# Reordering the prologue of a cross-attention kernel: value-bias sums, weight sums and the banks of the first queries

## The chip, the cores and the metric

The kernel runs on one core of a Trainium2 chip. The metric is device time in microseconds (us), the median of several executions. The engines are TensorE (PE in the profile, with PEld for its weight loads), VectorE (DVE), ScalarE (ACT), GpSimd (POOL) and SyncE (SP, which here only issues DMAs). Each engine works through its own queue in order, and semaphores hold an instruction until its data are there.

## The reference

One layer: layer norm, cross-attention with 8 heads of 64, a small recurrent state over time, and a row that is added at the end. All of it is float32.

```python
# builder_state x: (1, 4096, 512), base_state: (1, 3202, 512), program_probs: (1, 3202, 64)
x = _layernorm(builder_state, g1, beta1)
base_n = _layernorm(base_state, g1, beta1)
x = residual + _mha(x, base_n, W_qkv, b_qkv, W_o, b_o)   # softmax(q k^T / 8) v, 8 heads
xn = _layernorm(x, g2, beta2)
U = (xn @ W_in.T + b_in) @ Bmat
s = jax.nn.silu(s @ A.T) + u_t                           # a scan over the 4096 steps
x = x + einsum('tbs,sh->bth', states, Cmat)
return x + (program_probs.mean(axis=1) @ W_prog.T + b_prog)[:, None, :]
```

The gain g1 and the shift beta1 of the first layer norm are folded into the weights. For keys, values and queries each weight is multiplied by g1, and beta1 times the weight, summed over its rows, goes into the bias.

## The kernel before, in words

The work has a prologue and a main stage. The prologue makes all keys and values of the 3202 context rows, writes them to DRAM (`kd`, `vd`), makes the constants, and makes the first queries. The main stage goes over 8 blocks of 512 queries, 4 pairs of heads and 2 halves, and for each over 13 double chunks of keys: scores (L1067), exponential (L1144), sum (L1152), product with the values (L1201). The change is in the prologue, and nothing of the main stage's code is touched.

**Chunks and groups.** The context is cut into 26 chunks of 128 rows, loaded as `cx` (L426). A chunk is normalised: statistics on DVE (L267, L269), factors on POOL (L276, L278, L280), scaling on ACT (L288); for the first two chunks DVE scales (L440). It is then turned, by PE and a copy (L304, L456) or, for chunks 0 and 1 of groups 2 to 5, by DVE and DMAs (L407, L419). Chunks 0 to 3 make group 0, whose values (L540) and keys (L663) are plain products, one of values for each chunk and one of keys for each pair of heads. The groups 1 to 5 use a seven-product scheme for keys and values alike (`Seven`, L500): it needs sums of the weights, made once on POOL (`weight_sums`, L708, tiles `sk` and `sv`), and four differences of the turned chunks for each group, made on DVE (`t`, L735). Results are kept by ACT (L513, L517) and joined by DVE (the pieces named `tied`, L523).

**Bias sums.** `shift(k, after, due)` makes the bias of queries (k = 0), keys (1) or values (2). DVE multiplies the raw weight by beta1 and adds up four row blocks (L399 once, L402 three times; pieces `("wv", 0)` to `"wv.w"` for the values). PE sums over rows with eight one-column matmuls (L801, piece `"wv.pb"`), and DVE adds the given bias (L808, `"wv.bias"`). The keys' bias is needed when a key product is copied out (L673). The values' bias is needed only for `rowv`, a row of the output projection that comes late in the prologue. The gains themselves are L392: those of the values come before the plan starts, those of keys and queries are pieces (`gained`).

**The planner.** The function `lead` lists the prologue as pieces: name, engine, a cost in ns, what must come first (`after`), a due time, and rings of buffers taken and given. `Plan.order` plays the pieces through on a clock of its own. Whenever an engine is free, it takes the ready piece with the earliest due time, and the pieces are then emitted in that order. So `after`, `due` and costs decide the order in each engine's queue; on the chip only data and buffers hold an instruction back. Buffers of tiles that follow one another in a ring do so too: a chunk's load waits until the sixth chunk before it has been normalised.

The planner knows one more rule, the port. A POOL piece, or a DVE piece whose name's first part is in `PORT`, is not started on its clock before the last such piece is over:

```python
def shares(p):
    return p["engine"] == "POOL" or p["engine"] == "DVE" and p["name"][0] in self.PORT

def fits(p):
    if port > now and shares(p):
        return False
```

The due times that matter are: values of chunk c 4000 c, keys of head pair hp in group 0 14500 + 3560 hp, gains of the keys 9500, their bias 11500, statistics of chunks 4 and 5 22500 and their factors 24000, weight sums 9000 (values) and 16000 (keys), the column sum of a bias 4000 after the due time given to `shift`.

**The banks of PSUM.** Small products take their tile from `m_tile`, which goes round a list of pools: `ps_m` and `ps_p` in the prologue, one bank each; `ps_m` and `ps_n` in the main stage. Fourteen tiles come before the first query product in the prologue, which makes three products of the first queries (`heads`, L333, copied by L342): they stand in `ps_m`, `ps_p` and `ps_m`. The main stage begins with `sample` (L1087), which opens a tile in `ps_m` and one in `ps_n`. Its pools are opened after those of the prologue are closed, in the order `ps_s` (scores, four banks), `ps_n`, `ps_o` (two banks, the products with the values; the fourth query product uses the first of them).

Of the kernel before, what the change touches and what calls it, by code (L numbers as in the profile page):

```python
# [55 lines left out]
def keys(c):  # L56


    return CK if c < NCH - 1 else REST
# [11 lines left out]
class Plan:  # L71
# [9 lines left out]
    KEEP, ALONE = 6000, 30000  # L81
    UNIT = ("add", "inverse", "scale", "fall", "join", "output", "sums", "den", "swap", "gather", "fold", "rest")
    ENDS = 2 * NC * NQB - 2
    PORT = ("add", "rest", "fold", "gather", "scale")

    SHIFT = {
        "row.store": 11.5, "fold": 2, "rows.outs": 0.75, "heads": -12, "sample": -3, "spread": 4.75,
# [26 lines left out]
    def order(self):  # L114
# [13 lines left out]
        def shares(p):  # L128
            return p["engine"] == "POOL" or p["engine"] == "DVE" and p["name"][0] in self.PORT

# [61 lines left out]
def xattn_ssm_kernel(  # L192
# [66 lines left out]
    wq = kv.tile([P, NC, H], F32, name="wq")  # L259
# [52 lines left out]
    ps_m = actx.enter_context(tc.tile_pool(name="ps_m", bufs=1, space=PSUM))  # L312
    m_pools = [ps_m]

    def m_tile(shape, name):

        pool = m_pools.pop(0)
        m_pools.append(pool)
        return pool.tile(shape, F32, tag="m", name=name)
# [9 lines left out]
    def heads(Q, hp, xn, home=None):  # L329

        pq = home() if home else m_tile([P, 512], f"pq_{Q}_{hp}")
        for i in range(NC):
            nc.tensor.matmul(  # L333
                pq,
                wq[:, i, hp * P : (hp + 1) * P],
                xn[:, i, :],
                start=(i == 0),
                stop=(i == NC - 1),
            )
        yield  # L340
        t = qp.tile([P, QB], F32, tag="q", name=f"q_{Q}_{hp}")
        nc.scalar.activation(  # L342
            t, pq, AF.Identity, bias=bias[:, hp : hp + 1], scale=HD**-0.5
        )
        qt[Q, hp] = t
# [37 lines left out]
    wk = wp.tile([P, NC, H], F32, name="wk")  # L383
    wv = wp.tile([P, NC, H], F32, name="wv")
# [89 lines left out]
    def quarters(w):  # L474

        lo, hi = slice(0, QU), slice(QU, H)
        return w[:, :2, lo], w[:, 2:, lo], w[:, :2, hi], w[:, 2:, hi]
# [78 lines left out]
    def lead():  # L556
# [6 lines left out]
        add = plan.add  # L563
# [3 lines left out]
        def start_of(g):  # L567
            if g == n_g:
                return start_of(g - 1) + 10000
            return 31000 + (g - 1) * GROUP if g else 0  # L570

        def used(c):
            g, i = divmod(c, GC)
            if g == 0 or g == n_g:
                return start_of(g) + i * 4000
            return start_of(g) + (i > 1) * 4 * SLOT
# [16 lines left out]
        for c in range(1, NCH):  # L593
            u, n, g, v = used(c), keys(c), c // GC, {}
# [101 lines left out]
        def weight_sums(name, w, tags, after, due):  # L696

            a11, a12, a21, a22 = quarters(w)
            left = dict(zip("124", (a11, a12, a22)))
            tiles = {}  # L700

            def sum_(k, x, y, op):
                i = "57".index(k) if k in "57" else "63".index(k)
                if k in "57":
                    tiles[i] = xp_.tile([P, 2, H], F32, tag=tags[i], name=f"s{name}{k}", bufs=1 if name == "k" else 2)
                left[k] = tiles[i][:, int(k in "63")].rearrange("p (c o) -> p c o", c=2)
                x, y = (left[z] if isinstance(z, str) else z for z in (x, y))
                nc.gpsimd.tensor_tensor(left[k], x, y, op)  # L708

            for i, (k, x, y, op) in enumerate((  # L710
                ("5", a21, a22, ALU.add), ("6", "5", a11, ALU.subtract),
                ("7", a11, a21, ALU.subtract), ("3", a12, "6", ALU.subtract),
            )):
                first = {"6": "5", "7": "6", "3": "7"}.get(k)
                add(("s", name, k), "POOL", 1300, partial(sum_, k, x, y, op),
                    after + ([("s", name, first)] if first else []), due + i * 1300)
            return left
# [63 lines left out]
        def weighted_(name, w, by, after, due):  # L781
            v = sv_[name] = {}

            def run(i):
                if i == 0:
                    v["w"] = weighted(w, by, f"shift_{name}")
                v["t"] = next(v["w"])

            for i in range(NC):
                add((name, i) if i < NC - 1 else name + ".w", "DVE", 750 if i else 450, partial(run, i),  # L790
                    [(name, i - 1)] if i else after, due + i, [] if i else ["w"])

        def shift(k, after, due):
            name = "w" + "qkv"[k]
            weighted_(name, raw[k], be1s, after, due)
            v = sv_[name]

            def product():
                v["pb"] = m_tile([P, 512], f"pb_{k}")
                for o in range(NC):  # L800
                    nc.tensor.matmul(  # L801
                        v["pb"][:, o : o + 1], v["t"][:, o * P : (o + 1) * P], ones[:, 0:1],
                        start=True, stop=True,
                    )

            def sum_():
                cs = slice(k * NC, (k + 1) * NC)
                nc.vector.tensor_tensor(bias[:, cs], v["pb"][:, :NC], bqkv[:, cs], ALU.add)  # L808
                if k == 0:
                    nc.vector.tensor_scalar(bias[:, cs], bias[:, cs], HD**-0.5, None, ALU.mult)  # L810

            add(name + ".pb", "PE", 900, product, [name + ".w"], due + 4000, ["m"], [("w", (name, 0))])
            add(name + ".bias", "DVE", 300, sum_, [name + ".pb"], due + 5500, [], [("m", name + ".pb")])
# [3 lines left out]
        def fetched(name, issue, cost, after, due):  # L817
            add("d." + name, "ACT", 100, issue, after, due)
            arrives("in." + name, cost, ["d." + name])
# [5 lines left out]
        def issue(name, src, *shape, tag=None):  # L825
            return lambda: nc.scalar.dma_start(tile_(*shape, name=name, tag=tag), src)
# [6 lines left out]

        gained("wk", 1, wk, 9500)
        shift(1, ["in.wk"], 11500)
        shift(2, [], 18500)
        fetched("win", issue("win", w_in.rearrange("(c p) i -> p c i", p=P), P, NC, H, tag="raw_k"), 6000,
                ["wk.w", ("k", 0, 0)], 17000)
        fetched("bm", issue("bm", bmat.rearrange("(c p) s -> p c s", p=P), P, NC, NS), 1500, [("k", 0, 0)], 17100)
# [108 lines left out]
        for t in range(NT):  # L948
            name, v, d = f"x{t * P}", {}, 96000 + t * 12000
# [24 lines left out]
        for hp in range(FIRST):  # L974
            v, d = {}, start_of(n_g) + 10000 + 3000 * hp

            def head(hp=hp, v=v):
                v["g"] = heads(0, hp, first_xn["xn"])
                next(v["g"])

            add(("h0", hp), "PE", 3560, head,
                [("x.copy", t) for t in range(NT)] + ["wq", "wq.bias"], d, ["m", "q"])
            add(("h0.q", hp), "ACT", 690, lambda v=v: next(v["g"], None), [("h0", hp)], d + 3600, [],
                [("m", ("h0", hp))])
# [3 lines left out]
        for hp in range(NC):  # L988
            keys_(0, hp)
        lefts = [  # L990
            weight_sums("k", wk, ("x1", "xn2"), ["wk"], 16000), weight_sums("v", wv, ("x", "x"), [], 9000),
        ]
        for g in range(1, n_g):
            group(g, lefts)
# [14 lines left out]
    with tc.manual_schedule():  # L1009
        load_chunk(0)  # L1010
        nc.scalar.dma_start(g1s, g1)
        fetch_w(2, nc.scalar, slice(0, NC // 2))
        fetch_w(2, nc.sync, slice(NC // 2, NC))
        load_chunk(1)
        load_chunk(2)
        fetch_w(1, nc.sync)
        load_chunk(3)
        idle = m_tile([P, 512], "idle")
        nc.scalar.copy(bu, neg_half)
        for _ in range(11):  # L1020
            nc.tensor.matmul(idle[:, :P], a_t, a_t, start=True, stop=True)
        for t, src in ((be1s, beta1), (bqkv, b_qkv), (g2s, g2), (be2s, beta2)):
            nc.sync.dma_start(t, src)
        for c in range(4, 6):
            load_chunk(c)
        early = [first_chunk(c) for c in range(2)]
        next(early[0])
        next(early[0])
        turn_chunk(0)
        copy_chunk(0)  # L1030
        gain(2, wv, 0)
        gain(2, wv, 1)
        next(early[1])
        gain(2, wv, 2)
        xhs[2] = normalize(cxs.pop(2), CK, "c2", pool=cin)
        gain(2, wv, 3)
        next(early[1])
        lead()
# [107 lines left out]
    def add(w, c):  # L1146

        nb, t = blocks(c), w["s"][c]
        before = w["s"][0] if c == 1 else w["acc"]
        if c == 1:  # L1150
            w["acc"] = accp.tile([CK, 2, 2, QU], F32, tag="acc", name=f"acc_{w['name']}", bufs=3)
        nc.vector.tensor_tensor(  # L1152
            w["acc"][:, :, :nb, :], t[:, :, :nb, :], before[:, :, :nb, :], ALU.add
        )
# [1176 lines left out]
```

## Time and profile before

| | us |
|---|---|
| median of 3 runs | 1930.76 (1929.99 to 1931.4) |
| the profiled execution, its own time | 1930.1 |
| its span, first to last instruction | 1928.2 |
| PE busy in the span | 1907.7 (99%) |
| DVE busy | 1507.3 (78%) |
| ACT busy | 1173.5 (61%) |
| POOL busy | 227.7 (12%) |
| mean granted TensorE clock | 0.997 of full speed |

The span is what the profile's times are counted in; the profiled execution's own time is 1.9 us longer. Busy shares are an average over a prologue of some 205 us and the main stage after it. In a row of the timeline stand the start, the duration, engine and line, the operation, output and inputs with their shapes, the count, and in brackets the idle time just before with what ended it. Several instructions of a kind may be merged to one row, whose duration then runs from the first to the end of the last. Durations of matmuls contain the pipeline's fill, so the distance between two starts says more than the duration of one row.

### The profile page before, as it was taken

To read this page: it belongs to the slowest core of one execution; us is meant where nothing else is said; L and a number is where in the kernel's file an instruction comes from. 1 tells how busy PE (TensorE), PEld (TensorE's weight loads), DVE (VectorE), ACT (ScalarE), POOL (GpSimd) and SP (SyncE) were. 2 spreads that over 40 slices of the span, in tenths; PEclk is the share of its full clock that TensorE was granted. 3 is DMA by queue.
4 is the path that set the end of the run, shared out by engine and by line. 5 is a ranking of instruction groups with operands and counts; after the bars stand their busy time and mean duration, and the time that the engine had idled before them with its cause. 6 is when DMAs were issued, how large, how long until landed. Compare 5 with 4: busy or idle time off the path is not lost.

```text
span 1928.2 us, 67580 instructions
## 1 busy us (share of the span) xinstructions
PE 1907.7 (99%) x29296; PEld 1325.5 (69%) x29296; DVE 1507.3 (78%) x2035; ACT 1173.5 (61%) x1647; POOL 227.7 (12%) x378
## 2 busy tenths in 40 slices
PE   8999999999999999999999999999999999999997
PEld 4888678676667766666667666766666666766675
DVE  5652588688878887888868887888789886978877
ACT  2342576676656666667657665766666765766653
POOL 5110000001200120011100120012000110011105
PEclk9999999999999999999999999999999999999999
DMA  6654133133422243223413342224323342545577
GB/s 216 184 155 115 44 109 85 48 93 85 126 77 82 87 120 88 71 81 96 113 54 86 91 126 79 82 87 118 81 72 90 81 121 60 149 117 145 173 188 230
DMA packets 260762, 207.47 MB, mean 108 GB/s; under 512 B 94633, under 2 KB 233897, under 8 KB 260461
## 3 DMA queue, kind: packets, MB, share of 16 engines
q1 hardware_dynamic: 256440, 196.48, 35.8%
q10 hardware_dynamic: 4020, 6.62, 1.2%
q8 instruction: 232, 3.80, 0.8%
q14 instruction: 70, 0.57, 0.1%
HBM read 156.32 MB, written 29.88 MB: 97 GB/s over the span
## 4 chain that ended last, share of the span: by engine, by line


## 5 line engine op out<-in xcount | busy, mean ns | idle before, releaser
L1144 ACT ACTIVATE p<-s,shifts 128x1024 f32<-128x1024 f32 (+1 forms) x832 | 892.8, 1082 | 475.4 <-PE s L1067 458.8
L1152 DVE TENSOR_TENSOR acc<-p,acc 128x1024 f32<-128x1024 f32 (+1 forms) x704 | 832.6, 1183 | 135.6 <-ACT p L1144 99.9
L1067 PE MATMUL s<-q,k 64*64 64x256 f32 x12800 | 840.2, 377 | 0.2 <-ACT p L1144 0.2
L1201 PE MATMUL po<-p,v 64*64 64x256 f32 x12800 | 839.3, 377 | 0.0
L1067 PEld LDWEIGHTS s<-q,k 64*64 64x64 f32 x12800 | 502.9, 133 | 196.7 <-ACT p L1144 15.0
L1201 PEld LDWEIGHTS po<-p,v 64*64 64x64 f32 x12800 | 500.4, 133 | 181.8 <-issue 17.3
L1273 DVE RECIPROCAL rd<-rd 128x256 f32<-128x256 f32 (+1 forms) x64 | 110.1, 1722 | 70.8 <-ACT rd L1268 70.8
L1438 POOL TENSOR_TENSOR xr<-xr,rowb 128x512 f32<-128x512 f32 x30 | 40.7, 1365 | 998.4 <-DMA xr<-in_x_dram 608.2
L333 PE MATMUL pq<-xn,wq 128*128 128x512 f32 x248 | 110.5, 598 | 0.0
L1444 PE MATMUL pa<-wo,o 128*128 128x512 f32 x240 | 107.0, 599 | 0.0
L1152 DVE TENSOR_TENSOR acc<-p,p 128x1024 f32<-128x1024 f32 x64 | 78.2, 1222 | 10.1 <-ACT p L1144 9.8
L333 PEld LDWEIGHTS pq<-xn,wq 128*128 128x128 f32 x248 | 45.8, 190 | 55.8 <-issue 55.8
L1444 PEld LDWEIGHTS pa<-wo,o 128*128 128x128 f32 x240 | 44.4, 190 | 56.0 <-issue 56.0
L342 ACT ACTIVATE q<-pq,bias 128x512 f32<-128x512 f32 x31 | 21.3, 687 | 84.3 <-PE pq L333 84.3
L1176 DVE TENSOR_TENSOR acc<-swap,acc 64x256 f32<-64x256 f32 x126 | 55.5, 441 | 9.2 <-ACT swap L1171 7.5
L1171 ACT COPY swap<-acc 64x256 f32<-64x256 f32 x126 | 50.8, 404 | 8.6 <-DVE acc L1159 5.4
L1138 DVE TENSOR_TENSOR acc<-x,acc 2x256 f32<-2x256 f32 x128 | 53.1, 415 | 2.6
L1461 POOL TENSOR_TENSOR xr<-x,modb 128x512 f32<-128x512 f32 x30 | 38.2, 1273 | 120.1 <-DVE x L1457 120.1
L1159 DVE TENSOR_TENSOR acc<-acc 128x512 f32<-128x512 f32 x63 | 44.2, 701 | 1.4
L523 DVE TENSOR_TENSOR ks<-pky,ks 128x512 f32<-128x512 f32 x15 | 10.4, 692 | 43.4 <-PE pky L500 26.4
L1334 POOL TENSOR_SCALAR rstd_x<-mv_x 128x1 f32<-128x1 f32 x28 | 6.2, 220 | 321.3 <-DVE mv_x L1331 319.6
L517 ACT ACTIVATE ks<-pkx,bias 128x256 f32<-128x256 f32 x40 | 16.8, 471 | 42.5 <-PE pkx L500 26.0
(260 smaller groups left out, 1410.1 us busy)
## 6 DMA issues: line engine op xcount, KB each, us to landing
k<-kd SPq DMA_DIRECT2D x432, 128.0 KB, 2.5
v<-vd SPq DMA_DIRECT2D x432, 128.0 KB, 2.2
xn<-x SPq DMA_DIRECT2D x448, 32.0 KB, 1.9
xr<-in_x_dram SPq DMA_DIRECT2D x30, 256.0 KB, 3.1
x1d<-xr SPq DMA_DIRECT2D x30, 256.0 KB, 2.6
x<-in_x_dram SPq DMA_DIRECT2D x28, 256.0 KB, 3.6
cx<-in_ctx_dram SPq DMA_DIRECT2D x25, 256.0 KB, 4.4
kd<-ks SPq DMA_DIRECT2D x20, 256.0 KB, 2.3
```

The lines of the kernel that those rows point to most:

```text
L333: nc.tensor.matmul(pq, wq[:, i, hp * P : (hp + 1) * P], xn[:, i, :], start=(i == 0), stop=(i == NC - 1),)
L1067: nc.tensor.matmul(s[k0 : k0 + HD, a, b, :], kts[(*w["at"][:2], c)][r, b * CK + k0 : b * CK + k0 + HD], q[r], start=True, stop=True, skip_ ...
L1138: nc.vector.tensor_tensor(to[r], t[r], to[r], ALU.add)
L1144: nc.scalar.activation(t[:, :, :nb, :], w["ps"][c][:, :, :nb, :], AF.Exp, bias=w["shift"])
L1152: nc.vector.tensor_tensor(w["acc"][:, :, :nb, :], t[:, :, :nb, :], before[:, :, :nb, :], ALU.add)
L1159: nc.vector.tensor_tensor(acc[:, :, 0, :], acc[:, :, 0, :], acc[:, :, 1, :], ALU.add)
L1171: nc.scalar.copy(w["swap"][r], of[(1 - k) * HD : (2 - k) * HD])
L1176: nc.vector.tensor_tensor(of[r], w["swap"][r], of[r], ALU.add)
L1201: nc.tensor.matmul(w["po"][k][a * HD : (a + 1) * HD, :QU], vts[Q, hp, c][r, b, a * HD : (a + 1) * HD], t[r, a, b, :], start=(c == 0 and b ...
L1273: nc.vector.reciprocal(w["rd"][:, part], (w["pd"] if last else w["rd"])[:, part])
L1438: nc.gpsimd.tensor_tensor(v["x"], v["x"], rowb, ALU.add)
L1444: nc.tensor.matmul(v["pa"], o_t[Q, c, half][:, t * P : (t + 1) * P], wo[:, c, :], start=(c == 0), stop=(c == NC - 1),)
```

## The change

Four edits, all in the planner's inputs for the prologue. First, the names `t`, `tied`, `wk`, `wv`, `wq` and `rowv` join `PORT`: the differences, the joins and the multiply-and-add pieces of the bias sums (all but the last of each four, whose names are plain strings) are kept apart from POOL's pieces on the planner's clock. Second, the value-bias sums come after the first key product, `("k", 0, 0)`, with due time 24000 instead of 18500; before they had no predecessor. Third, the weight sums of the values come after the statistics of chunk 5, due 20000 instead of 9000; before they had no predecessor. Fourth, when the first of the first query products is issued, the list of pools is sorted so that `ps_m` comes last; the three products then stand in `ps_p`, `ps_m` and `ps_p`.

```diff
-    PORT = ("add", "rest", "fold", "gather", "scale")
+    PORT = ("add", "rest", "fold", "gather", "scale", "t", "tied", "wk", "wv", "wq", "rowv")
...
         shift(1, ["in.wk"], 11500)
-        shift(2, [], 18500)
+        shift(2, [("k", 0, 0)], 24000)
...
             def head(hp=hp, v=v):
+                if hp == 0:
+                    m_pools.sort(key=lambda pool: pool is ps_m)
                 v["g"] = heads(0, hp, first_xn["xn"])
                 next(v["g"])
...
-            weight_sums("k", wk, ("x1", "xn2"), ["wk"], 16000), weight_sums("v", wv, ("x", "x"), [], 9000),
+            weight_sums("k", wk, ("x1", "xn2"), ["wk"], 16000), weight_sums("v", wv, ("x", "x"), [("c.stats", 5)], 20000),
```

## Prediction

> **What bounds the kernel now.** I read the page first, for who is busy, then a table of stretches, for where TensorE (PE) is not.
>
> ```profile
> span 1928.2 us, 67580 instructions
> ...
> PE 1907.7 (99%) x29296; PEld 1325.5 (69%) x29296; DVE 1507.3 (78%) x2035; ACT 1173.5 (61%) x1647; POOL 227.7 (12%) x378
> ```
> ```profile
> 13.11:28.20 15.09, 10.08 (x24) 5.38 (x25) 14.59 (x22) 3.51 (x5) 12.24 (x15) 0.77 0.41 112
> ...
> 47.69:195.00 147.31, 147.31 (x719) 122.20 (x718) 66.41 (x124) 51.86 (x96) 20.65 (x60) 1.00 0.53 151
> 195.00:205.00 10.00, 9.13 (x37) 4.98 (x41) 0.68 (x1) 3.17 (x6) 0.37 (x2) 1.00 0.21 59
> 205.00:1928.20 1723.20, 1710.95 (x28426) 1176.03 (x28418) 1411.66 (x1852) 1105.89 (x1525) 180.60 (x267) 1.00 0.36 101
> ```
>
> In the stretches the columns are start and end, length, then busy time of PE, weight loads, DVE (VectorE), ACT (ScalarE) and POOL (GpSimd), granted clock, DMA share, GB/s. PE is busy in all of 47.69 to 195 us and in 1710.95 of the 1723.20 us after 205. So what follows the prologue cannot get shorter by this change; it can only begin earlier. There are two holes the change could touch: 13.11 to 28.20, where PE has 10.08 us of work in 15.09 and the clock is 0.77, and a short one near 204. The waits of PE name both.
>
> ```profile
> PE pb L801 <- DVE shift_wv L402: 5.0, 1, 5.0
> ...
> PE pv L540 <- ACT ct L456: 0.8, 2, 0.5
> ```
> ```profile
> PE sm L1087 <- ACT q L342: 0.9, 1, 0.9
> ```
>
> The timeline shows the first hole (start, duration, instruction).
>
> ```profile
> 10.35 0.73 DVE L440 TENSOR_SCALAR xh_c<-cx,mv_c,rstd_c 128x256 f32<-128x256 f32 x2
> ...
> 11.45 0.60 PE L304 MATMUL tp_c<-ident,xh_c 128*128 128x128 f32 x4
> 11.51 1.27 POOL L708 TENSOR_TENSOR sv<-wv 128x512 f32<-128x512 f32 x1
> ...
> 12.21 0.85 DVE L399 TENSOR_SCALAR shift_wv<-raw_v,be1s 128x512 f32<-128x512 f32 x1 [1.13 <-DMA be1s<-in_L_xattn_beta_dram]
> ...
> 12.45 0.66 PE L304 MATMUL tp_c<-ident,xh_c 128*128 128x128 f32 x4 [0.40 <-ACT xh_c L288]
> ...
> 13.09 4.97 DVE L402 SCALAR_TENSOR_TENSOR shift_wv<-raw_v,be1s,shift_wv 128x512 f32<-128x512 f32 x3
> ...
> 15.81 1.70 POOL L708 TENSOR_TENSOR sv<-wv,sv 128x512 f32<-128x512 f32 x1
> 17.99 0.68 DVE L456 COPY ct<-tp_c 128x512 f32<-128x512 f32 x1
> 18.12 1.87 PE L801 MATMUL pb<-ones,shift_wv 128*128 128x1 f32 x8 [5.01 <-DVE shift_wv L402]
> ...
> 19.85 8.94 PE L540 MATMUL pv<-wv,ct 128*128 128x512 f32 x16
> ```
> ```profile
> 28.63 1.04 PE L304 MATMUL tp_c<-ident,xh_c 128*128 128x128 f32 x8
> ```
>
> PE turns chunks 1 and 2 by 13.11 and then stands until 18.12: next in its queue is the column sum of the value bias (L801). That waits for three DVE instructions that took 4.97 us, and behind them stands the copy of chunk 1 (17.99) that the next values need. Two things stretch the hole. The same three instructions for the queries, with POOL still, took 2.33, against 4.97 beside POOL's sums; and after the pause the clock is half.
>
> ```profile
> 17.00:18.00 1.00, 0.00 (x0) 0.00 (x0) 1.00 (x2) 0.00 (x0) 0.51 (x1) 0.50 0.00 0
> ```
> ```profile
> 33.49 3.60 PE L663 MATMUL pk<-ct,wk 128*128 128x512 f32 x8
> ...
> 36.92 0.95 PE L801 MATMUL pb<-ones,shift_wk 128*128 128x1 f32 x8
> ...
> 37.73 10.55 PE L663 MATMUL pk<-ct,wk 128*128 128x512 f32 x24
> ...
> 39.57 0.48 DVE L399 TENSOR_SCALAR shift_wq<-raw_q,be1s 128x512 f32<-128x512 f32 x1
> ...
> 40.09 2.33 DVE L402 SCALAR_TENSOR_TENSOR shift_wq<-raw_q,be1s,shift_wq 128x512 f32<-128x512 f32 x3
> ```
>
> **The change, part by part.** *Value-bias sums.* They leave the front of the queues: DVE's four (L399, L402) and PE's eight (L801) now come after the first key product. They issue no DMA. What is late next? Chunk 1's copy: its turn ends at 11.45 + 0.60 = 12.05, DVE has been free since 10.35 + 0.73 = 11.08, and 0.68 for the copy gives 12.8; PE is still turning chunk 2 until 13.11. So the values of chunk 1 start at 13.11 instead of 19.85. Eight warm matmuls of this shape take 36.92 - 33.49 = 3.43 us, two chunks 6.87, and chunk 3 can be turned at about 20.0 instead of 28.63: **8.6 us**. The eight column sums come back later, in a stretch where PE is full: 37.73 - 36.92 = **0.8 us** lost. I take no cost for DVE's four: at 0.48 + 2.33 they end long before PE reaches their sum, behind the fourth key product (due time 28,000 against 25,180 for that product). The most they could cost is the rival "early sum" below.
>
> Is chunk 3 there at 20.0, and are the key weights there at 33.49 - 8.6 = 24.9?
>
> ```profile
> 3.29 0.62 SPq L426 DMA_DIRECT2D cx<-in_ctx_dram  x1
> ```
> ```profile
> DMA to landing us min/median/max: 8.7/8.7/8.7
> ```
> ```profile
> 18.59 0.68 DVE L267 BATCH_NORM_STATS2 st_c<-cx 128x6 f32<-128x512 f32 x1
> ...
> 19.30 0.18 DVE L269 BATCH_NORM_AGGREGATE mv_c<-st_c 128x2 f32<-128x6 f32 x1
> ...
> 20.84 0.81 ACT L288 ACTIVATE xh_c<-cx,nmr_c,rstd_c 128x512 f32<-128x512 f32 x1 [7.11 <-POOL nmr_c L280]
> ...
> 21.16 1.64 DVE L392 TENSOR_SCALAR wk<-raw_k,g1s 128x512 f32<-128x512 f32 x4
> ```
>
> Chunk 3 lands at 12.0. From its statistics to the end of its normalising took 18.59 to 21.65, 3.1 us, in a contended place. Begun at 12.8 it ends near 15.9: four us of slack. The DMA engines move nothing at 17 to 18, so everything asked for early, the key weights too, has landed by 17; four gains at 1.64 end by 18.7, six us ahead. Both covers hold; if one failed, each us late would be a us of PE.
>
> *Weight sums.* POOL's four sums of wv (L708) move from 11.5 to behind chunk 5's statistics. By their due times (20,000 for wv, 16,000 for wk) all eight sums pass ahead of chunk 5's factors (24,000), so chunk 5 and those behind it in POOL's queue are made later, and so is SP's load of chunk 11, which waits for chunk 5's buffer. Eight at 1.27 to 1.70 take 10 to 14 us; begun near 16 they end by 30, chunk 5 is normalised by 33 (3.1 as above), and PE wants it after the fourth key product, which ended at 47.69, so at 47.69 - 8.6 = 39.1 or later. Cost nothing, 6 us of cover.
>
> *GpSimd and VectorE exclude each other.* The planner keeps some DVE pieces and all of POOL's apart on its own clock. No wait is added to the program: only orders change. A piece that would be run beside POOL is passed over, and another goes ahead of it. Where they collide the trace puts 4.97 against 2.33, so up to 2.6 us of DVE for three instructions could be gained; PE is full from 28 on, so a gain there is worth nothing. The other side is the rival "t late". I take zero.
>
> [...]
>
> *First queries.* The hole near 204:
>
> ```profile
> 200.41 0.69 ACT L342 ACTIVATE q<-pq,bias 128x512 f32<-128x512 f32 x1 [3.02 <-PE pq L333]
> 203.84 0.69 ACT L342 ACTIVATE q<-pq,bias 128x512 f32<-128x512 f32 x1 [2.75 <-PE pq L333]
> ...
> 204.68 0.78 PE L1087 MATMUL sm<-q,kx 64*64 64x256 f32 x8 [0.87 <-ACT q L342]
> ```
>
> The sample (L1087) uses queries copied long before; it waits for the PSUM bank. Fourteen tiles before them alternate between two banks, so query products 0 and 2 stand in ps_m, which the sample opens first. Swapped, product 2 stands in ps_p and ps_m's reader is the copy at 200.41, over by 201.1. ps_p's bank becomes, by order of allocation, the last of the main stage's (ps_o's second), written only at the first value product. So the wait goes: between 0, if the bank meets another early tile, and **0.87**. I take 0.87.
>
> Sum: 8.6 - 0.8 + 0.87 = 8.7 us. The profiled execution took 1930.1 us (span 1928.2), so 1921.4; the median of the three runs, 1930.76, lies 0.66 above that execution. **Forecast: 1922.1 us.**
>
> **The rivals.** *t late* (chance 0.20). In the five groups PE's products wait for differences that DVE makes (t, L735), with hardly any room:
>
> ```profile
> 113.38 0.69 DVE L735 TENSOR_TENSOR t<-ct 128x512 f32<-128x512 f32 x1
> ```
> ```profile
> 114.13 1.99 PE L500 MATMUL pky<-t,sk 128*128 128x256 f32 x8
> ```
>
> t ends at 114.07, its product begins at 114.13. If the planner holds t back while POOL has a piece, DVE takes statistics first, 0.68 and the aggregate, 0.86 in all. Once in each of five groups is 4.3 us: 1926.4. Against it: POOL is busy in only 20.65 of 147.31 us there, and the planner knows t's new time and can order PE otherwise.
>
> *Not apart after all* (0.12). The program holds no exclusion, so POOL's sums may still fall on DVE's gains or key-bias sums. Fully in turn, one gain and one sum are 0.41 + 1.27 = 1.7 us, four 6.7: key weights at 17 + 6.7 = 23.7 against 24.9, still hidden; with statistics placed between (two at 0.86) 0.5 late. Add as much again for the clock and a lost swap: about 1924.
>
> *Early sum* (0.10, the slow side). PE's column sum of the value bias is placed ahead of the second key product instead of behind the fourth, because in the planner that product isn't ready. PE gets there at 28.3 + 0.8 = 29.1. If DVE has the query gains (1.64) and the query shift (0.48 + 2.33) in front of wv's four (0.85 + 4.97 beside POOL), it ends 10.3 us later: PE stands that long and loses the clock again, which cost 8.78 - 6.87 + 0.92 = 2.8 us in the trace (19.85 to 28.63 for two chunks; 1.87 against 0.95). 1922.1 + 13.1 = 1935. It decides by its place in PE's queue: behind the fourth product PE arrives at 39.4, when 29.1 + 10.3 is just over. Due times speak for the late place; parts of it (a 5 us wait) would end near 1930.
>
> **How the numbers follow.** Forecast 0.58 (its own range 1920.5 to 1924, the lower end if PE's short waits for copies in the first 30 us, 0.8 in all, go too); t late 0.20; not apart 0.12; early sum 0.10. The range to 1927 takes in the first three and leaves early sum and the worst of t late out: 1920.5 to 1927. A measurement of this kernel can tell about 0.2%, 3.9 us, from no change. Below 1926.9 lie forecast, not apart and two thirds of t late: 0.83; within 0.2%: 0.09; slower: 0.08.
>
> **What would show it.** Right: no wait of PE for shift_wv, values of chunk 1 starting near 13.1, clock 1.00 throughout 13 to 28, first key product near 25, group stages full, no wait of sm for q. Then the 205 us mark falls near 196 and the rest lasts the same 1723 us. Wrong: PE waits on t or on shift_wv at a new place; a clock of 0.50 after 13; chunk 3 or the key weights late; or the main stage longer than 1723 us, for which no step above has a reason.

## The result, and the profile after

| | before | after |
|---|---|---|
| median of 5 runs, us | 1930.76 (1929.64 to 1931.56) | 1921.45 (1919.92 to 1922.86) |
| ratio, 95% interval | | 0.9952 (0.9937 to 0.9966) |
| profiled execution, own time, us | 1930.1 | 1919.92 |

The kernel became 9.3 us faster: 1921.45 us, where 1922.1 was forecast. The head of the page of the changed kernel:

```profile
span 1918.0 us, 67581 instructions
...
PE 1903.8 (99%) x29296; PEld 1318.5 (69%) x29296; DVE 1502.4 (78%) x2035; ACT 1173.6 (61%) x1647; POOL 231.5 (12%) x378
```

The table of stretches, with the columns as in the prediction:

```profile
13.11:28.20 15.09, 14.80 (x44) 7.05 (x42) 10.95 (x18) 4.65 (x8) 14.03 (x15) 1.00 0.75 223
41.65:188.59 146.94, 146.94 (x718) 122.13 (x717) 66.12 (x123) 51.76 (x97) 20.51 (x60) 1.00 0.53 151
188.59:198.00 9.41, 9.41 (x67) 4.61 (x65) 0.92 (x3) 1.90 (x4) 0.18 (x1) 1.00 0.17 49
198.00:1918.00 1720.00, 1708.21 (x28382) 1169.34 (x28378) 1406.36 (x1849) 1105.85 (x1525) 182.61 (x267) 1.00 0.36 101
```

In the stretch that held the hole PE now has 14.80 us of work where it had 10.08, and the clock is 1.00 where it was 0.77. The timeline of PE and DVE shows the steps:

```profile
11.24 0.60 PE L304 MATMUL tp_c<-ident,xh_c 128*128 128x128 f32 x4
11.87 0.69 DVE L456 COPY ct<-tp_c 128x512 f32<-128x512 f32 x1 [1.01 <-PE tp_c L304]
12.23 0.66 PE L304 MATMUL tp_c<-ident,xh_c 128*128 128x128 f32 x4 [0.40 <-ACT xh_c L288]
...
12.73 7.03 PE L540 MATMUL pv<-wv,ct 128*128 128x512 f32 x16
...
19.55 5.00 DVE L402 SCALAR_TENSOR_TENSOR shift_wk<-raw_k,be1s,shift_wk 128x512 f32<-128x512 f32 x3
19.60 1.04 PE L304 MATMUL tp_c<-ident,xh_c 128*128 128x128 f32 x8
...
24.46 3.60 PE L663 MATMUL pk<-ct,wk 128*128 128x512 f32 x8
...
29.47 2.33 DVE L402 SCALAR_TENSOR_TENSOR shift_wv<-raw_v,be1s,shift_wv 128x512 f32<-128x512 f32 x3
...
39.09 0.95 PE L801 MATMUL pb<-ones,shift_wv 128*128 128x1 f32 x8
...
39.90 0.63 PE L304 MATMUL tp_c<-ident,xh_c 128*128 128x128 f32 x4
...
41.65 1.89 PE L500 MATMUL pkx<-ct,wk 128*128 128x256 f32 x8
```

The values of chunks 1 and 2 start at 12.73, right behind chunk 1's copy; chunks 3 and 4 are turned at 19.60 instead of 28.63, and the first keys come at 24.46 instead of 33.49. The column sum of the value bias stands behind the fourth key product. Near the end of the prologue:

```profile
195.55 0.66 PE L1089 MATMUL sm<-q,kx 64*64 64x256 f32 x8
195.66 0.69 ACT L342 ACTIVATE q<-pq,bias 128x512 f32<-128x512 f32 x1 [2.75 <-PE pq L333]
```

The sample starts while the third query product is still to be copied; its wait is gone. (The lines behind the edited code are two higher than before.)

A ledger from the two timelines, each stretch from the start of one row to the start of the next, in us:

| stretch | before | after | difference |
|---|---|---|---|
| start of the span to first key product | 33.49 | 24.46 | -9.03 |
| on to the first product of group 1 (pkx from ct) | 16.35 | 17.19 | +0.84 |
| on to the last two query products of the prologue | 146.94 | 146.94 | 0.00 |
| on to the sample | 7.90 | 6.96 | -0.94 |
| on to the main stage's first value product (po) | 7.96 | 7.85 | -0.11 |
| on to the end of the span | 1715.56 | 1714.60 | -0.96 |

The first five add up to -9.24. The last is the spread of executions: over the thirteen profiles of this study, whose main stage is the same code, it lies between 1714.6 and 1719.1 us. The clock may be part of it: in port_alone, banks_alone, port_bias, port_diff and sums_warm, which took 1717.3 to 1719.1 here, the mean granted clock of the whole span was 0.996, 0.996, 0.998, 0.998 and 0.998, in the other eight, with 1714.6 to 1717.4, it was 0.997 to 0.999. The spread is larger than most prices below. So the tables give the **po mark** (the start of the first value product of the main stage) beside the times: up to there two profiles differ by some tenths of a us where only orders off the critical path differ (212.64 and 212.74 for before and port_alone; at the first keys 33.49 and 33.82 for before and banks_alone, whose edit comes only later).

### The profile page after: what moved, and what is told of

It reads as the page before. It is cut to its first block, busy times and chain, and to the rows that moved or that the text cites. A ratio compares the mean times of both kernels' runs of the same rounds, so it can differ in the third digit from the quotient of the medians.

```text
span 1918.0 us, 67581 instructions
## 1 busy us (share of the span) xinstructions
PE 1903.8 (99%) x29296; PEld 1318.5 (69%) x29296; DVE 1502.4 (78%) x2035; ACT 1173.6 (61%) x1647; POOL 231.5 (12%) x378
## 4 chain that ended last, share of the span: by engine, by line
```

## The experiments

The theory, as the prediction has it: the move of the value-bias sums makes the gain, by taking PE's 5 us wait and the half clock away; the weight sums' move and the exclusion are worth nothing; the bank swap is worth 0.9 us. The rival: the gain needs several of the edits together.

| kernel | median, us (runs) | ratio, 95% interval | first keys | po mark |
|---|---|---|---|---|
| before (its profile) | | 1 | 33.49 | 212.64 |
| bias_alone | 1926.49 (11) | 0.9979 (0.9970 to 0.9988) | 27.17 | 207.16 |
| sums_alone | 1927.96 (11) | 0.9981 (0.9972 to 0.9990) | 31.13 | 210.32 |
| port_alone | 1931.33 (11) | 0.9999 (0.9990 to 1.0008) | 33.57 | 212.74 |
| banks_alone | 1931.57 (11) | 1.0000 (0.9991 to 1.0009) | 33.82 | 211.91 |
| after | 1921.45 (5) | 0.9952 (0.9937 to 0.9966) | 24.46 | 203.40 |
| after less the sums' move: sums_front | 1926.93 (9) | 0.9975 (0.9965 to 0.9985) | 28.94 | 207.87 |
| after less the exclusion: no_port | 1924.17 (5) | 0.9963 (0.9949 to 0.9976) | 24.29 | 205.10 |
| after less t and tied: port_bias | 1923.38 (5) | 0.9956 (0.9943 to 0.9970) | 24.47 | 203.67 |
| after less the bias sums' names: port_diff | 1924.07 (5) | 0.9961 (0.9948 to 0.9975) | 24.57 | 205.92 |
| after less the swap: no_banks | 1921.89 (5) | 0.9953 (0.9939 to 0.9967) | 24.47 | 204.51 |
| before, hole filled: warm_fill | 1930.02 (11) | 0.9993 (0.9984 to 1.0002) | 30.83 | 209.97 |
| sums_alone, hole filled: sums_warm | 1926.34 (10) | 0.9972 (0.9963 to 0.9981) | 28.04 | 208.95 |

Ratios are to the kernel before on the same chip (its medians there were 1931.23, 1931.65 and 1931.68).

### The value-bias sums alone

```diff
-        shift(2, [], 18500)
+        shift(2, [("k", 0, 0)], 24000)
```

> The kernel before with one edit: the value-bias sums come after the first key product. Theory (the place in the queues makes the hole, the collision with GpSimd and the half clock only stretch it): the hole closes by itself; chunk 3 is turned at about 20.0 us instead of 28.63, the first key product starts near 24.9, 0.8 us come back behind the fourth key product: 1930.8 - 7.8 = 1923.0 us, and the sample still waits 0.9 us for q. GpSimd's value-weight sums stay in front (11.3 to 16.4 us), so chunk 3's factors come at about 17 and its scaled rows by 18.8, 1.2 us ahead of need. Rival (GpSimd's sums hold the prologue): chunk 3 is late by their length, turned at 22 or later: 1925 us or more.

Measured: 4.7 us gained instead of about 8, a **miss** of the theory. PE's wait of 5.0 is gone, and the clock is 1.00 from 10 to 28 us, but the timeline has two new waits:

```profile
15.04 1.45 POOL L708 TENSOR_TENSOR sv<-wv,sv 128x512 f32<-128x512 f32 x1
16.93 0.67 POOL L278 TENSOR_TENSOR rstd_c<-ve_c,neg_half 128x1 f32<-128x1 f32 x1
...
18.92 1.05 POOL L278 TENSOR_TENSOR rstd_c<-ve_c,neg_half 128x1 f32<-128x1 f32 x1
...
20.49 0.81 ACT L288 ACTIVATE xh_c<-cx,nmr_c,rstd_c 128x512 f32<-128x512 f32 x1 [1.55 <-POOL nmr_c L280]
...
21.36 0.66 PE L304 MATMUL tp_c<-ident,xh_c 128*128 128x128 f32 x4 [1.23 <-ACT xh_c L288]
...
23.00 1.07 ACT L456 COPY ct<-tp_c 128x512 f32<-128x512 f32 x2
```
```profile
23.63 3.70 PE L540 MATMUL pv<-wv,ct 128*128 128x512 f32 x8 [1.61 <-ACT ct L456]
```

Follow it backwards. PE turns chunk 4 right behind chunk 3, ahead of chunk 3's values. Chunk 4 was scaled on ACT only at 20.49, since its factors on POOL came after the four sums of wv (the last ends at 16.49) and chunk 3's factors. And ACT, which holds chunk 3's copy too, gets to it only at 23.00, behind the scalings of chunks 4 and 5. PE waits 1.23 + 1.61 us, and the first keys come at 27.17, 2.7 us later than in the changed kernel, where POOL makes chunk 4's factors first and the sums after them:

```profile
14.79 0.22 POOL L276 TENSOR_SCALAR ve_c<-mv_c 128x1 f32<-128x1 f32 x1
...
15.94 0.70 POOL L280 TENSOR_SCALAR nmr_c<-mv_c,rstd_c 128x1 f32<-128x1 f32 x1
...
16.61 1.27 POOL L708 TENSOR_TENSOR sv<-wv 128x512 f32<-128x512 f32 x1
```

### The weight sums alone

```diff
-            ... weight_sums("v", wv, ("x", "x"), [], 9000),
+            ... weight_sums("v", wv, ("x", "x"), [("c.stats", 5)], 20000),
```

> The kernel before with one edit: GpSimd's sums of the value weights come after chunk 5's statistics. Theory (place and collision both): VectorE's four instructions of the value bias still stand before chunk 1's copy, but take 0.48 + 2.33 = 2.8 us instead of 5.8; TensorE waits about 2 us instead of 5.0, too short to lose the clock; values of chunk 1 start at 15.9 instead of 19.85, chunk 3 is turned at 22.7 instead of 28.63: 1930.8 - 5.9 = 1924.9 us. Rival 1 (place alone, the collision is nothing): 1930.8. Rival 2 (collision alone makes the hole): all of it, about 1922.5.

Measured: 3.3 us by the medians, 2.3 by the po mark, against 6 expected. With POOL still, DVE's three pieces of the value bias take 2.33 instead of 4.97, and PE's wait falls from 5.0 to 2.0, as expected. But the clock does not hold. The timeline, then slices with the granted clock as third column from the end:

```profile
15.04 1.70 PE L801 MATMUL pb<-ones,shift_wv 128*128 128x1 f32 x8 [2.04 <-DVE shift_wv L402]
16.61 9.82 PE L540 MATMUL pv<-wv,ct 128*128 128x512 f32 x16
26.27 1.04 PE L304 MATMUL tp_c<-ident,xh_c 128*128 128x128 f32 x8
```
```profile
15.00:16.00 1.00, 0.96 (x6) 0.96 (x6) 1.00 (x2) 0.00 (x0) 0.00 (x0) 0.62 0.85 272
...
22.00:23.00 1.00, 1.00 (x4) 0.52 (x3) 1.00 (x1) 0.00 (x0) 1.00 (x2) 0.96 0.68 244
```

The fall, at 15.24, came behind a pause of 2.04 us (that this would be too short to lose the clock was the author's estimate): two chunks of values took 9.66 us instead of 6.87, and the column sums 1.57 instead of 0.81 (from start to start). What the shorter wait gave (3 us), the clock kept back in part: it stayed at 0.50 while PE was busy throughout, in 6.00 of the 6.00 us from 16 to 22.

### The exclusion alone and the swap alone

```diff
-    PORT = ("add", "rest", "fold", "gather", "scale")
+    PORT = ("add", "rest", "fold", "gather", "scale", "t", "tied", "wk", "wv", "wq", "rowv")
```

> The kernel before with one edit: the names added to PORT. Theory (the exclusion is only in the planner's clock, the program holds no wait): at the front of the queues the order stays, value-bias sums and GpSimd's sums still run side by side, 4.97 us for the three instructions, TensorE waits 5.0: 1930.8 us, within 1. Rival (the two engines are really kept apart): 2.33 us for the three, a wait near 2 us, 1925 us. Second rival (differences of the groups are pushed back, 0.86 us in each of five groups): 1935 us, with TensorE waiting for t.

Measured: no change, as the theory had it. The wait of PE stands where it stood:

```profile
PE pb L801 <- DVE shift_wv L402: 5.0, 1, 5.0
```

```diff
+                if hp == 0:
+                    m_pools.sort(key=lambda pool: pool is ps_m)
```

> The kernel before with one edit: the list of pools is sorted before the first of the first query products. Theory: the sample's wait of 0.87 us for q goes and nothing takes its place: 1930.8 - 0.9 = 1929.9 us; in the profile the sample follows the last of the three query products at once. Rival: another early tile of the main stage (scores or first value product) waits for the same bank instead, 1930.8 us, with a new wait of up to 0.87 us between the sample and the first value product.

Measured: nothing that the times could tell, and in the profile the sample's wait is gone; from the last two query products to the po mark it is 14.81 us instead of 15.86.

```profile
204.07 0.66 PE L1089 MATMUL sm<-q,kx 64*64 64x256 f32 x8
204.17 0.69 ACT L342 ACTIVATE q<-pq,bias 128x512 f32<-128x512 f32 x1 [2.75 <-PE pq L333]
```

### One edit taken out of the changed kernel

By the po marks the four edits alone give 5.5, 2.3, -0.1 and 0.7 us, 8.4 in all, against 9.24 together; that near-sum hides that they are not independent, as the next runs show. (The move of the value-bias sums was not taken out of the changed kernel by itself.)

The weight sums back at the front:

```diff
-            ... weight_sums("v", wv, ("x", "x"), [("c.stats", 5)], 20000),
+            ... weight_sums("v", wv, ("x", "x"), [], 9000),
```

> The changed kernel with one part undone: the value-weight sums have no predecessor and due time 9000 again, so GpSimd does them before the factors of chunks 3 and 4. Theory (the hole closes only if the sums leave GpSimd's front too): as with the value bias moved alone, TensorE waits 1.2 us for chunk 4's scaled rows and 1.6 us for chunk 3's copy behind them, the first key product starts near 27.2 instead of 24.5: 1921.5 + 2.7 = 1924.2 us. Rival (the three other edits carry the gain, and the waits with the bias moved alone came from an order that PORT or the banks mend): 1921.5.

Measured: 4.47 us later at the po mark. PE's two waits are those of bias_alone, 1.21 and 1.61. In this execution they cost the clock as well, which they did not in the other:

```profile
21.43 0.66 PE L304 MATMUL tp_c<-ident,xh_c 128*128 128x128 f32 x4 [1.21 <-ACT xh_c L288]
23.70 5.40 PE L540 MATMUL pv<-wv,ct 128*128 128x512 f32 x8 [1.61 <-ACT ct L456]
28.94 3.60 PE L663 MATMUL pk<-ct,wk 128*128 128x512 f32 x8
```
```profile
24.00:24.50 0.50, 0.50 (x2) 0.10 (x2) 0.00 (x0) 0.14 (x1) 0.50 (x2) 0.56 1.16 357
...
27.00:27.50 0.50, 0.50 (x2) 0.30 (x1) 0.00 (x0) 0.00 (x0) 0.42 (x2) 0.52 1.01 389
```

So with everything else in place the sums' move is worth 4.5 us where the clock falls and some 2.8 where it does not: chunk 3's values took 5.24 us here (28.94 - 23.70) and 3.54 in bias_alone.

The exclusion taken out:

```diff
-    PORT = ("add", "rest", "fold", "gather", "scale", "t", "tied", "wk", "wv", "wq", "rowv")
+    PORT = ("add", "rest", "fold", "gather", "scale")
```

> The changed kernel with one part undone: PORT as before. Theory (the exclusion gives nothing to the time): 1921.5 us within 1.5, chunk 3 turned near 19.6 and the first key product near 24.5, as in the changed kernel. Rival (it keeps collisions away from the path): slower by 1 to 3 us, with TensorE waiting for VectorE (a gain, a bias or t).

Measured: 1.70 us later at the po mark (the times, 2.7 us apart, don't settle it: the intervals overlap). A second **miss** of the theory. The waits of PE, then ACT's and POOL's timeline:

```profile
PE pk L663 <- ACT ks L673: 1.6, 1, 1.6
```
```profile
30.48 0.81 ACT L288 ACTIVATE xh_c<-cx,nmr_c,rstd_c 128x512 f32<-128x512 f32 x1 [5.36 <-POOL nmr_c L280]
...
32.38 0.81 ACT L288 ACTIVATE xh_c<-cx,nmr_c,rstd_c 128x512 f32<-128x512 f32 x1 [1.09 <-POOL nmr_c L280]
33.10 0.67 ACT L673 ACTIVATE ks<-pk,bias 128x512 f32<-128x512 f32 x1
```
```profile
27.25 1.26 POOL L708 TENSOR_TENSOR sk<-wk,sk 128x512 f32<-128x512 f32 x1
...
30.05 0.40 POOL L280 TENSOR_SCALAR nmr_c<-mv_c,rstd_c 128x1 f32<-128x1 f32 x1
```

The third key product needs a PSUM bank from which ACT has to copy the first keys. ACT could do so at 28.9, when the bias is there, but its queue has the scalings of chunks 5 and 6 in front, and these wait for factors that POOL makes behind its eight sums. ACT stands idle for 5.36 us. In the changed kernel ACT's queue has the first keys first (29.08) and chunk 5's scaling behind them (29.66). So the exclusion's gain is an **order on ACT**, an engine that it does not name. That this order comes about because the exclusion puts POOL's pieces later on the planner's clock is read from the planner's rule, not shown by a run.

Which of the names do it? Two halves of the list:

```diff
+    PORT = ("add", "rest", "fold", "gather", "scale", "wk", "wv", "wq", "rowv")
```

> The changed kernel with only the names of the bias sums (wk, wv, wq, rowv) in the exclusion; t and tied taken out again. Theory (what the exclusion is worth is the order on ACT: with it the copy of the first keys stands ahead of the scaling of chunks 5 and 6, and it is the names of the bias sums that set this order): as the changed kernel, 1921.5 us, ACT's copy of the first keys starts near 29.1 as soon as its bias is there, no wait of PE at the third key product, first added-feature product near 41.7. Rival (t and tied, the names of the differences and of the slices of the main stage, carry it): 1923 to 1924 us, PE waits 1.6 us for ACT's ks at the third key product, first added-feature product near 43.4.

```diff
+    PORT = ("add", "rest", "fold", "gather", "scale", "t", "tied")
```

> The changed kernel with only t and tied added to the exclusion, the names of the bias sums taken out again. Theory (the names of the bias sums set the order on ACT): as without any of the added names, 1923 to 1924 us, PE waits 1.6 us at the third key product for ACT's ks, which starts near 33 behind two scalings, and the first added-feature product starts near 43.4. Rival (t and tied carry it): 1921.5 us, no such wait, first added-feature product near 41.7.

Measured: the times are 0.7 us apart and settle nothing; the profiles do. With the bias sums' names ACT copies the first keys at once and the first product of group 1 starts at 41.66, as in the changed kernel (41.65); ACT's row:

```profile
29.09 0.69 ACT L673 ACTIVATE ks<-pk,bias 128x512 f32<-128x512 f32 x1 [3.78 <-DVE bias L808]
```

With t and tied alone PE waits as without any name:

```profile
34.12 7.13 PE L663 MATMUL pk<-ct,wk 128*128 128x512 f32 x16 [1.62 <-ACT ks L673]
```

So the bias sums' names set this order. What t and tied add is not settled: with them the po mark is 0.27 us earlier (203.40 against 203.67) beside the other names, and 0.82 later (205.92 against 205.10) without them. Of the 0.82, 0.28 stands already at the first keys, and in the groups PE's one listed wait is 0.3 us for ACT's copy of values, none for t.

The swap taken out:

```diff
-                if hp == 0:
-                    m_pools.sort(key=lambda pool: pool is ps_m)
```

> The changed kernel with the banks of the first queries not swapped. Theory (the swap takes away the wait of the score product for the copy of the second query, 0.87 us in the prediction, and nothing else): marks up to the last query product as in the changed kernel, first score product 7.9 us behind the first of the last query products instead of 7.0, the mark of the first output product 0.9 to 1.1 us later, 1922.4 us. Rival (the swap is worth nothing once the first keys come earlier): the same marks as the changed kernel, 1921.5 us.

Measured: 1.11 us later at the po mark, and the sample waits again; in the times it does not show.

```profile
196.50 0.82 PE L1087 MATMUL sm<-q,kx 64*64 64x256 f32 x7 [0.87 <-ACT q L342]
```

### The clock by itself

In the kernel before, and in sums_alone, matmuls whose result nobody uses were put into PE's queue ahead of the column sum of the value bias, 20 and 8 of them. They add work and remove none. (The profile lists each of these float32 matmuls twice: 20 in the code are x40, and the x8 of a column sum are four.)

```diff
             def product():
+                for _ in range(20 if k == 2 else 0):
+                    nc.tensor.matmul(idle[:, :P], a_t, a_t, start=True, stop=True)
```

> The kernel before with 20 matmuls of zeros (128x128, into the idle tile) in TensorE's queue just ahead of the column sum of the value bias, so that it works through most of its 5 us wait. The wait for VectorE's sums stays. Theory (the pause costs a half clock on top of itself): the clock stays at 1.00, the column sum takes 0.95 instead of 1.87 us, the values of chunks 1 and 2 take 6.9 instead of 8.8 us: 1931.2 - 2.8 = 1928.4 us. Rival (the half clock is no part of the loss): 1931.2.

> The kernel with the value-weight sums moved alone, and 8 matmuls of zeros (128x128, into the idle tile) ahead of the column sum of the value bias, to fill the 2.0 us wait. Theory (that kernel fell short of its 1924.9 us because even a 2 us pause lost the clock): the clock stays at 1.00, the column sum takes 0.95 instead of 1.70 us, the values of chunks 1 and 2 take 6.9 instead of 9.7 us, the first key product starts at 27.7 instead of 31.13: 1928.0 - 3.4 = 1924.6 us. Rival (it is VectorE's or GpSimd's lateness that made these products slow): 1928.0, with the same starts.

Measured, in the kernel before:

```profile
12.91 4.63 PE L800 MATMUL idle<-a_t 128*128 128x128 f32 x40
18.10 1.05 PE L803 MATMUL pb<-ones,shift_wv 128*128 128x1 f32 x8 [0.56 <-DVE shift_wv L402]
19.02 7.11 PE L540 MATMUL pv<-wv,ct 128*128 128x512 f32 x16
25.97 1.04 PE L304 MATMUL tp_c<-ident,xh_c 128*128 128x128 f32 x8
```

PE reaches the column sum at the same 18.1, but the two chunks take 25.97 - 19.02 = 6.95 us and the clock is 1.00 from 13 to 23 us: 2.67 us are won at the po mark (2.8 expected). The times (1.6 us less than before by the medians, 1 inside the interval) don't show it. In sums_warm the clock is 1.00 from 13 to 23 us too, the first keys come at 28.04 instead of 31.13, near the 27.7 expected, and 1.4 us remain at the po mark; of the rest 0.35 is lost before group 1 and 1.41 in the groups, where PE lists two waits of 0.4 for ACT's copies. So of the 9.03 us up to the first keys, about 2.7 were the clock, 5.2 the wait, 0.9 the column sum itself (at full clock, it comes back later) and 0.2 an earlier start of this execution.

## Why the prediction was right

**Value-bias sums.** Right in mechanism, order and size: 8.6 us forecast, 9.03 measured. The values start at 12.73 instead of 13.11: this execution's prologue runs 0.22 us earlier (chunk 2's turn starts at 12.23 instead of 12.45), and the product starts 0.50 us behind the start of that turn, while the prediction had waited for the turn's modelled end, 0.66 behind. From there on, the 6.87 us to the turn of chunk 3 came out exactly. The column sum's 0.8 us came back as 39.90 - 39.09 = 0.81, behind the fourth key product, and DVE's four were done by 31.8, seven us before PE asked (39.09): the rival *early sum* did not occur.

**Weight sums.** "Cost nothing" held, but it was the wrong question. The prediction looked at chunk 3 and at chunk 5 and those behind it, and never at chunk 4, whose turn stands ahead of chunk 3's values in PE's queue (the row of x8 that it quotes holds both). Without it chunk 4's factors are late: 2.7 us at the first keys in bias_alone, 4.5 with the clock in sums_front. "Four us of slack" for chunk 3 was true with POOL free: it was normalised by 15.6 in the changed kernel (15.9 forecast), and by 18.9 in bias_alone, 0.6 us ahead of its turn. The forecast came out because the move of the sums, taken for a neutral one, supplied this slack and chunk 4's; as far as chunk 4 goes that was luck, since the prediction never looked at it.

**GpSimd and VectorE exclude each other.** Taken as zero, because PE was thought to be full from 28 on; in the changed kernel it is worth 1.7 us, by ACT's order: without it PE stands still for 1.6 us at the third key product. Alone it is worth nothing. *t late* did not occur: from 41.65 to 188.59 PE is busy in all 146.94 us, and no wait of PE is listed there. *Not apart after all* was right as to the fact and harmless: the key-bias pieces at 19.55 took 5.00 us beside POOL's sums, and PE's sum of them is asked for only at 27.89.

One such piece took 5.00 / 3 = 1.67 us beside POOL's sums here and 2.33 / 3 = 0.78 at 29.47, without them; the sums that ran beside these pieces took 1.46 to 1.71 us, and the last two, with DVE idle, 1.26 and 1.27. One after the other in full, 0.78 and 1.27 would be 2.05, so the "fully in turn" of this rival is an assumption that no run shows.

**First queries.** 0.87 forecast, 0.94 up to the sample and 1.05 to 1.11 up to the po mark; the last 0.1 to 0.2 is spread over the rows behind the sample and was not followed.

So the total, 8.7 forecast and 9.24 measured up to the po mark, is right step by step in what it removes. What failed is the pricing of two parts at zero: without the one the po mark is 4.5 us later, without the other 1.7.

## What to carry to other kernels

When a change removes a wait, list every instruction that stands behind it in that engine's queue up to the goal, and check the supplier of each one; here the products next in the queue were in time, and the turn of chunk 4 behind them was late without the second edit. Price an edit in a bundle by taking it out of the bundle, and not only by making it alone: the exclusion gave nothing alone and 1.7 us in company. And where a planner orders the queues, a cost or a rule for one engine moves the order on others: read the queue of the engine that nobody named.

## What the runs showed of the hardware

From slices of three profiles the edges of the prologue's half clock can be read. In sums_alone the slices above put the fall at 15.24 (0.62 in 15 to 16 is 0.24 us at full and 0.76 at half) and the return at 22.08, 6.84 us later. For the kernel before:

```profile
16.00:17.00 1.00, 0.00 (x0) 0.00 (x0) 0.96 (x2) 0.00 (x0) 1.00 (x1) 0.86 0.14 43
...
23.00:24.00 1.00, 1.00 (x3) 0.36 (x2) 0.95 (x2) 0.70 (x1) 0.92 (x2) 0.73 0.70 234
```

16.72 to 23.54, 6.82 us. In sums_front it is 24.06 to 27.48, 3.42 us, half of that.

In the 3.42 us ahead of the fall PE had no work in before (13.30 to 16.72), 0.98 us of matmuls in sums_alone (0.12 + 0.66 + 0.20) and 1.02 in sums_front (0.66 + 0.36). So the clock fell in two of the three although PE had not stood still for all of these 3.42 us.

Nearly the same pair of pauses lost the clock in sums_front (1.21 and 1.61 us) and not in bias_alone (1.23 and 1.61). First bias_alone, then sums_front:

```profile
21.00:22.00 1.00, 0.64 (x4) 0.42 (x4) 0.86 (x4) 0.97 (x3) 0.90 (x3) 1.00 0.06 21
22.00:23.00 1.00, 0.02 (x1) 0.00 (x0) 0.90 (x4) 1.00 (x3) 1.00 (x1) 1.00 0.69 59
23.00:24.00 1.00, 0.37 (x1) 0.30 (x2) 0.52 (x1) 1.00 (x3) 0.92 (x1) 1.00 0.96 323
```
```profile
20.65:24.06 3.41, 1.01 (x5) 0.72 (x6) 2.06 (x6) 3.38 (x6) 3.15 (x5) 1.00 0.62 163
```

In bias_alone PE is busy for 0.64 + 0.02 + 0.37 = 1.03 us in the three slices and stands still from 20.14 to 21.00, which makes 1.03 us in the 3.42 up to 24.00; the clock is 1.00 in every slice up to 30 us. In sums_front PE is busy for 1.01 us in the 3.41 ahead of the fall at 24.06. Busy time alone does not tell the two apart, and what does is not shown by these runs.
